# A macaron block on one core: the order of work in an attention step, one small copy moved to another engine, fewer products of constants

## The chip, the cores and the metric

The kernel runs on one core of a Trainium2 chip. The metric is the device time of one execution in microseconds, as the median of several runs. The engines named below are TensorE (PE, with its weight loads PEld), VectorE (DVE), ScalarE (ACT), GpSimd (POOL) and SyncE (SP), which here only issues DMAs.

## What is computed

The input `x` has 4 sequences of 2048 tokens with 256 features, so 8192 tokens, all float32. The block is a macaron: half a mixture-of-experts layer, attention, and half a mixture-of-experts layer again, with the same weights in both halves.

```python
x = x + 0.5 * ffn(layernorm(x))
x = x + attention(layernorm(x))
x = x + 0.5 * ffn(layernorm(x))

def attention(x):                      # H = 16 heads of 16 features
    s = (16 ** 0.5) ** -0.25
    q = split_heads(x @ Wq + bq)
    v = split_heads(x @ Wv + bv)
    q = softmax(q, axis=-1) * s        # over the 16 features of a head
    k = softmax(q, axis=-2) * s        # over the 2048 tokens, from q
    ctx = einsum('bhnd,bhne->bhde', k, v)
    return merge(einsum('bhnd,bhde->bhne', q, ctx)) @ Wo + bo
```

`ffn` routes each token to 2 of 8 experts by a softmax over `x @ router_w.T`. An expert takes at most 1280 tokens, those with the largest weights first. It computes `(silu(x @ wg) * (x @ wu)) @ wd` with 1024 hidden features, and the weighted results are added to the token's row.

## The kernel before

**Stages.** In the profiled execution the first router and the routing take the first 103 us. The first experts' products run from about 107 to 922 us, attention from 922 to 1160 us, the second routing to about 1223 us, and the second experts to the end. The experts gather the rows of their tokens with indirect DMAs on GpSimd's queue (`gather`), transpose them on TensorE, multiply, and scatter the results with indirect DMAs.

**Products of constants.** `stay_busy(out, n, cols)` issues n matrix products of constants that nothing reads. There are seven of them ahead of attention. In each of the two experts' stages there are four of 512 columns behind the first two gathers, and one of 384 columns behind each of the first two transposes of gathered rows.

**Attention in tiles and pairs.** The 8192 tokens are 64 tiles of 128 tokens; a tile is one slice `xw[:, t, :]` in SBUF. Two tiles make a pair, so there are 32 pairs (`NP`), and 8 pairs make a sequence (`PB`). The tiles are loaded from DRAM four at a time (`JL`), by 16 DMAs of 512 KB on SP's queue, in order. Besides the 256 features a tile of `xw` has 8 more columns: `wqx` is `Wq` with the router's weights beside it, so that the projection of the unnormalized tile also gives its part of the next router's logits (`W1` is 264 columns).

**The loop.** `attention` runs a loop of 44 steps. It stands in a manual schedule, so every engine executes its instructions in the order in which they are written, and no planner moves them. Step `i` works on several pairs at once, each at its own stage:

- `stats(2i+2)`: mean and variance of the next pair on VectorE; GpSimd makes the reciprocal deviation `rstd`.
- `turn_x(i)`: four transposes of the pair (`trx`) on TensorE, and a ScalarE copy out of PSUM to `xT`.
- `project(i-1)`: eight products into `qp` (PSUM, one buffer).
- `logits_in(i-1)`: a ScalarE copy of 128x16 logits from `qp` into `xw`.
- `largest(i-1)`: VectorE scales `qp` into `q` (two instructions) and takes the largest value of each head (`m`); GpSimd subtracts it from `q` in place.
- `exp(i-2)`: the exponential of `q` on ScalarE, in place. `share(i-2)`: VectorE sums each head (`z`) and takes the reciprocal (`rz`); GpSimd multiplies `q` by it in place. Here `q` holds the softmax.
- `keys(i-3)`: ScalarE takes a second exponential, `ek`, and scales the two tiles of the pair by `rstd` into a ring of four buffers (`xs`).
- `turn_q(i-3)`: four transposes of `q` (`trq`) and a ScalarE copy to `qT`.
- `sums(i-3)`: eight products of `ek` and `xs`, added up in `pc` over the 8 pairs of a sequence.
- `add_y(i-12)`: eight products of `qT` and the sequence's context `mo` into `py` (PSUM, one buffer until the last pairs). `take_y`: VectorE adds `py` to `xw`, takes the new statistics, and every second time the normalization constants (`norm_of`).
- `choose_on`: VectorE's part of the routing of finished tiles (`choose`), in small portions, from step 20 on.

When the 8 pairs of a sequence are summed, four parts make its context. `context_1` (steps 11, 19, 27, 35) takes the reciprocal `rc` on VectorE and scales `pc` into `g`, half on ScalarE and half on VectorE. `context_2` transposes `g` (`trg`) and copies it to `gT` on ScalarE. `context_3` multiplies it by the weights of `v` (`ctx`) and scales it on VectorE. `context_4`, in the next step, multiplies by `Wo` and makes `mo`.

**Buffers.** `trx`, `trq`, `trg` and `ctx` share the tag `tr`, which has two PSUM buffers. They are handed out in the order in which the code asks for them, and each comes free when the copy of its contents has been made. The tag `q` has five buffers in SBUF, `m` and `z` three.

**Order within a step.** The body of the loop sets it. Before the change it is: `context_1`, `context_4`, `exp`, `turn_x`, `share`, `stats`, `project`, `logits_in`, `keys`, `context_2`, `largest`, `turn_q`, `add_y`, `context_3`, `sums`, `choose_on`, `take_y`. In the sequence with the last context (step 35) portions of `choose_on` stand between them.

Of the kernel before, what the change touches and what calls it, by code (L numbers as in the profile page):

```python
# [26 lines left out]
def macaron_kernel(  # L27
# [22 lines left out]
    nc = tc.nc  # L50
# [3 lines left out]
    T = B * NJ  # L54
# [96 lines left out]
    def stay_busy(ps, n, cols=BANK):  # L151

        for _ in range(n):
            nc.tensor.matmul(ps[:, :cols], ident, row_of_ones[:, :cols], start=True, stop=True)

    def spread(ap, shape):
        return ap.to_broadcast(shape)
# [280 lines left out]
    def experts(name, src, dst, wait_for, weights, wpool, pool, ppool):  # L438
# [33 lines left out]
        def turn(k, q):  # L472

            if k >= len(chunks):
                return
            if q == 0:
                turned[k] = xTs[k] = pool.tile([P, DC, CH * P], F32, tag="xsT", name="xsT", bufs=2)
            c, i0, i1 = q // 2, (0, TURN)[q % 2], (TURN, CH)[q % 2]
            ps = ppool.tile([P, BANK], F32, tag="tr", name="tr", bufs=1)
            for i in range(i0, i1):  # L480
                nc.tensor.transpose(  # L481
                    ps[:, (i - i0) * P : (i - i0 + 1) * P], got[k][i][:, c * P : (c + 1) * P], ident
                )
                if k == 0 and c == 0 and i + 1 < TURN:
                    stay_busy(banks()[:, 0, :], 1, BANK * 3 // 4)
            nc.scalar.copy(turned[k][:, c, i0 * P : i1 * P], ps[:, : (i1 - i0) * P])

        def tt(o, a, b, op):
# [26 lines left out]
        def banks():  # L515

            return ppool.tile([P, 2, BANK], F32, tag="mm", name="mm", bufs=3)
# [138 lines left out]
        with tc.manual_schedule(engines=ENGINES - {mybir.EngineType.Pool}):  # L656
            first.high()
            first.begin()
            for g in range(NL):
                first.low(g)  # L660
                first.products(g)
            first.sum()
            lists[0] = first.end()
            gather(0)
            gather(1)
            stay_busy(banks()[:, 0, :], 4)
            for m in range(2):
                sums_of_w(0, m)
            blank(0, *range(TURN))
            for q in (0, 2):  # L670
                turn(0, q)
            for k, (e, i0) in enumerate(chunks):
                for p, hs in enumerate(steps_of(k)):
                    beside(k, p)

                order = [(i, p, j) for i in range(CH) for p in range(NF) for j in range(2)]
                order = sorted(order[: 4 * NF], key=lambda o: (o[1] == NF - 1, o[0])) + order[4 * NF :]
                po = {}
                for i, p, j in order:
                    if i not in po:  # L680

                        po[i] = banks()[:, 0, :D]
                    nc.tensor.matmul(  # L683
                        po[i], hs[p][:, j, i * P : (i + 1) * P], weights[e][2][:, j * NF + p, :],
                        start=(p == 0 and j == 0), stop=(p == NF - 1 and j == 1),
                    )
                    if i == CH - 1 and (p, j) == (NF // 2, 0):
                        behind(k, i - 0.5)
                    if p < NF - 1 or j == 0:
                        continue  # L690
                    eo = pool.tile([P, D], F32, tag="eo", name="eo", bufs=6)
                    nc.scalar.mul(eo, po[i], got[k][i][:, D + e : D + e + 1])  # L692
                    ins = nc.gpsimd.indirect_dma_start(  # L693
                        out=dst[:, :],
                        out_offset=bass.IndirectOffsetOnAxis(ap=lists[e][:, i0 + i : i0 + i + 1], axis=0),
                        in_=eo, in_offset=None, compute_op=ALU.add,
                    )
                    tc.declare_no_dep(ins.ins, group=f"{name}{e}", reason="an expert's rows are distinct")
                    tc.add_to_no_dep_group(f"{name}{e}", ins.ins)
                    after(ins, sent[e - 1], "the rows' earlier sums")  # L700
                    sent.setdefault(e, []).append(ins)
                    behind(k, i)
                del got[k]
                if i0 + CH == ST:
                    load_expert(e + 2, wpool, weights)
# [68 lines left out]
    def attention(xw, w, to, weights, pool, ppool):  # L774
# [34 lines left out]
                    )  # L809
            del xT[i]  # L810

        def logits_in(i):
            nc.scalar.copy(xw[:, 2 * i : 2 * i + 2, D:W1], qp[i][:, :, D:W1])

        def largest(i):
            q = pool.tile([P, 2, D], F32, tag="q", name="q", bufs=5)
            for k in range(2):
                nc.vector.scalar_tensor_tensor(  # L818
                    q[:, k, :], qp[i][:, k, 0:D], rstd[:, 2 * i + k : 2 * i + k + 1], bqs, ALU.mult, ALU.add
                )  # L820
            qs[i] = q.rearrange("p k (h d) -> p (k h) d", d=H)
            m = pool.tile([P, 2 * H], F32, tag="m", name="m", bufs=3)
            nc.vector.tensor_reduce(m, qs[i], AX.X, ALU.max)  # L823
            nc.gpsimd.tensor_tensor(qs[i], qs[i], spread(m.unsqueeze(2), [P, 2 * H, H]), ALU.subtract)  # L824

        def exp(i):
# [9 lines left out]
        def keys(i):  # L836


            eks[i] = pool.tile([P, 2, D], F32, tag="ek", name="ek", bufs=3)
            nc.scalar.activation(  # L840
                eks[i].rearrange("p k (h d) -> p (k h) d", d=H), qs[i], AF.Exp, scale=QSCALE
            )
            for k in range(2):
                t = 2 * i + k
                nc.scalar.mul(ring[i % 4][:, k, 0:D], xw[:, t, 0:D], rstd[:, t : t + 1])

        def turn_q(i):
            ps = ppool.tile([P, DC, 2, P], F32, tag="tr", name="trq", bufs=2)
# [119 lines left out]
        def has(i, n=NP):  # L968
            return 0 <= i < n

        LAST = NP + PB + 4
        with tc.manual_schedule(engines=ENGINES):
            stay_busy(ppool.tile([P, 2, 2 * D], F32, tag="py", name="py", bufs=1)[:, 0, :], 7)
            stats(0, 2)
            for i in range(LAST):
                y = i - PB - 4

                b3 = (i - 3) // PB - 1 if (i - 3) % PB == 0 else -1
                b4 = (i - 4) // PB - 1 if (i - 4) % PB == 0 else -1
                if has(b3, B):  # L980
                    context_1(b3)
                if b3 == B - 1:
                    choose_on(1, 0)
                if has(b4, B - 1):
                    context_4(b4)
                if has(i - 2):
                    exp(i - 2)
                if has(i):
                    turn_x(i)
                if has(i - 2):  # L990
                    share(i - 2)
                if has(i + 1):
                    stats(2 * i + 2, 2)
                if has(i - 1):
                    project(i - 1)
                    logits_in(i - 1)
                if has(i - 3):
                    keys(i - 3)
                if has(b3, B):
                    context_2(b3)  # L1000
                if b3 == B - 1:
                    choose_on(1, 0)
                if has(i - 1):
                    largest(i - 1)
                if has(i - 3):
                    turn_q(i - 3)
                ps = add_y(y) if has(y) else None
                if b3 == B - 1:
                    choose_on(3, 0)
                if has(b3, B):  # L1010
                    context_3(b3)
                if b3 == B - 1:
                    choose_on(2, 0)
                    context_4(b3)
                if has(i - 3):
                    sums(i - 3)
                if i < LAST - PB - 2:
                    choose_on(2, 2)
                if has(y):
                    take_y(y, ps)  # L1020
                if i >= LAST - PB:

                    choose_on({LAST - 3: 0, LAST - 2: 5, LAST - 1: 3}.get(i, 4), 0)
            while choosing:
                for k in reversed(range(len(choosing))):
                    choose_on(1, 0, k)
            for ts, _, tiles in chosen:
                for t in tiles:
                    norm_row(xw, t)
                write_rows(xw, to, ts)  # L1030
# [98 lines left out]
    xw = kept.tile([P, T, W], F32, name="xw")  # L1129
    w = kept.tile([P, E, T], F32, name="w")  # L1130
    with tc.tile_pool(name="at", bufs=1) as pool, tc.tile_pool(name="atp", bufs=1, space=PSUM) as ppool:
        for t in range(0, T, JL):
            nc.sync.dma_start(out=xw[:, t : t + JL, 0:D], in_=acc_tiles[:, t : t + JL, :])
        attention(xw, w, rows[1], att_weights, pool, ppool)


# [41 lines left out]
```

## Time and profile before

| what | value |
|---|---|
| time, median of 3 runs | 2049.84 us (2045.59 to 2050.16) |
| profiled execution: its own time | 2049.3 us |
| profiled execution: span of the trace | 2047.4 us |
| granted TensorE clock, mean | 0.959 of full speed |
| PE busy | 1891.1 us (92% of the span) |
| PEld busy | 1443.5 us (71%) |
| DVE busy | 1413.7 us (69%) |
| POOL busy | 883.5 us (43%) |
| ACT busy | 656.7 us (32%) |

The span is the time from the first to the last recorded instruction of the execution; 1.9 us of the execution's own time lie around it. Busy shares are averages over all stages, and the stages have different limits. In the experts' stages PE's slices of the span are at 90% or more, while in the attention stage (slices 19 to 23 of 40) they are lower at the beginning and in the routing behind it. So the change has to be read from the trace of the attention stage, step by step, and not from these totals. In a row of the trace a line such as L827 is the line of the program that issued the instruction, and `out<-in` gives the names of its tiles.

### The profile page before, as it was taken

Reading aid. Unit: us, or ns where it says so; the run is one execution under the profiler, and the core shown is the slowest. Engines: PE = TensorE matmul, PEld = TensorE weight load, DVE = VectorE, ACT = ScalarE, POOL = GpSimd, SP = SyncE. Lnnn points to the kernel's source line nnn. Section 1 sums busy time; section 2 is a strip of 40 time slices with the busy share of each in tenths; the row PEclk is TensorE's granted clock in tenths of the full one; section 3 lists DMA queues with packets and bytes.
Section 4 is the critical chain, followed back from the end, with each engine's and each line's share of the span. In section 5 each row is a group of like instructions: output and inputs, shape, how many; then the busy total and the mean of one; then the engine's idle time right before and its main releaser. Section 6 shows DMA issues by size and latency. Waiting matters only on the chain.

```text
span 2047.4 us, 24768 instructions
## 1 busy us (share of the span) xinstructions
PE 1891.1 (92%) x9200; PEld 1443.5 (71%) x9200; DVE 1413.7 (69%) x2499; ACT 656.7 (32%) x1357; POOL 883.5 (43%) x737
## 2 busy tenths in 40 slices
PE   6289999999999999997999628999999999999998
PEld 4257777777777777775888415777777777777776
DVE  7867676767676767545789886767676766767654
ACT  5322323222223222224566503222322222223221
POOL 5335353535353535334556303535353535353533
PEclk8579999999999999999999858999999999999999
DMA  9912222222231322115012531223132323131211
GB/s 350 298 28 38 78 38 78 40 77 64 52 79 37 79 40 39 18 16 169 21 42 86 181 136 28 71 45 79 37 79 40 81 37 83 35 84 35 42 15 13
DMA packets 99911, 147.63 MB, mean 72 GB/s; under 512 B 7496, under 2 KB 86352, under 8 KB 99664
## 3 DMA queue, kind: packets, MB, share of 16 engines
q1 hardware_dynamic: 69056, 102.77, 14.9%
q0 software_dynamic: 30720, 43.27, 13.0%
q8 instruction: 73, 1.20, 0.3%
q14 instruction: 46, 0.38, 0.1%
q10 hardware_dynamic: 16, 0.01, 0.0%
HBM read 98.84 MB, written 55.57 MB: 75 GB/s over the span
## 4 chain that ended last, share of the span: by engine, by line
PE 82%; DVE 7%; POOL 2%; issue 1%; ACT 1%; DMA 1%; POOLq 0%; SPq 0%; DVEq 0%; ACTq 0%
PE mm L536 41%; PE mm L683 27%; PE one L536 7%; PE tr L481 2%; PE ix L404 1%; PE py L922 1%; DVE above L303 1%; PE pc L864 1%; PE qp L807 1%; DVE q L818 1%; POOL q L824 1%; DVE m L823 1%; DVE z L831 1%; DVE st L934 0%; DVE st L791 0%
## 5 line engine op out<-in xcount | busy, mean ns | idle before, releaser
L683 PE MATMUL mm<-wdt,h 128*128 128x256 f32 x2560 | 579.0, 381 | 0.0
L683 PEld LDWEIGHTS mm<-wdt,h 128*128 128x128 f32 x2560 | 475.9, 190 | 63.9
L568 POOL TENSOR_TENSOR h<-ct 128x1280 f32<-128x1280 f32 x96 | 279.2, 2908 | 423.6 <-ACT ct L565 420.4
L536 PE MATMUL mm<-xs,ws 128*128 128x320 f32 x1536 | 459.5, 435 | 2.0 <-DVE xs L489 2.0
L489 DVE TENSOR_TENSOR ct<-ct,mm 128x640 f32<-128x640 f32 x384 | 313.1, 818 | 104.3 <-PE mm L536 96.2
L536 PEld LDWEIGHTS mm<-xs,ws 128*128 128x128 f32 x1536 | 292.4, 191 | 127.4 <-issue 6.6
L565 ACT ACTIVATE ct<-ct 128x320 f32<-128x320 f32 (+1 forms) x224 | 181.8, 812 | 283.7 <-DVE ct L489 283.7
L489 DVE TENSOR_TENSOR ct<-p,mm 128x640 f32<-128x640 f32 x128 | 105.1, 821 | 238.5 <-ACT p L553 200.5
L489 DVE TENSOR_TENSOR ct<-u,mm 128x640 f32<-128x640 f32 x256 | 210.3, 821 | 58.3 <-PE mm L536 55.3
L553 ACT COPY p<-one 128x320 f32<-128x320 f32 x256 | 108.8, 425 | 406.2 <-PE one L536 404.0
L693 POOL DMA_INDIRECT out_dram<-eo,ixs x80 | 133.1, 1664 | 220.7 <-ACT eo L692 213.7
L693 POOL DMA_INDIRECT acc<-eo,ixs x80 | 132.8, 1660 | 221.1 <-ACT eo L692 214.1
L456 POOL DMA_INDIRECT r<-rows,ixs x160 | 159.1, 994 | 145.4 <-DVE ws L489 97.3
L692 ACT ACTIVATE eo<-mm,r 128x256 f32<-128x256 f32 x160 | 75.9, 474 | 396.3 <-PE mm L683 396.3
L536 PE MATMUL mm<-xsT,ws 128*128 128x320 f32 x512 | 158.7, 432 | 0.0
L395 DVE TENSOR_TENSOR lo<-count,slot_lo 128x1024 f16<-128x1024 int16 x112 | 128.3, 1218 | 0.0
L536 PEld LDWEIGHTS mm<-xsT,ws 128*128 128x128 f32 x512 | 97.3, 190 | 40.5
L489 DVE TENSOR_TENSOR u<-p,mm 128x640 f32<-128x640 f32 x128 | 104.9, 820 | 16.4 <-PE mm L536 13.3
L536 PE MATMUL mm<-xsT,wgt 128*128 128x320 f32 x256 | 91.0, 437 | 0.0
L536 PE MATMUL one<-xsT,wgt 128*128 128x320 f32 x256 | 91.0, 437 | 0.0
L536 PE MATMUL mm<-xsT,wut 128*128 128x320 f32 x256 | 90.9, 437 | 0.0
L536 PE MATMUL one<-xsT,wut 128*128 128x320 f32 x256 | 90.1, 434 | 0.0
(211 smaller groups left out, 2333.6 us busy)
## 6 DMA issues: line engine op xcount, KB each, us to landing
wgt<-in_L_ffn_wg_dram SPq DMA_DIRECT2D x16, 1024.0 KB, 5.0
wut<-in_L_ffn_wu_dram SPq DMA_DIRECT2D x16, 1024.0 KB, 7.0
wdt<-in_L_ffn_wd_dram SPq DMA_DIRECT2D x16, 1024.0 KB, 5.6
rows<-xw SPq DMA_DIRECT2D x7, 2176.0 KB, 11.1
xw<-in_L_attn_x_dram SPq DMA_DIRECT2D x16, 512.0 KB, 8.9
xw<-acc SPq DMA_DIRECT2D x16, 512.0 KB, 8.8
out_dram<-xw SPq DMA_DIRECT2D x16, 512.0 KB, 2.9
r<-rows,ixs POOLq DMA_INDIRECT x160
```

Source lines behind the costliest of these rows:

```text
L303: nc.vector.tensor_scalar(above, wt, cand_f, 0.0, ALU.is_ge, ALU.add, accum_out=part)
L395: nc.vector.tensor_tensor(lo, spread(count.unsqueeze(1), shape), spread(at.unsqueeze(2), shape), ALU.is_equal)
L456: nc.gpsimd.indirect_dma_start(out=r, out_offset=None, in_=src[:, :], in_offset=bass.IndirectOffsetOnAxis(ap=lists[e][:, i : i + 1], axis=0),)
L481: nc.tensor.transpose(ps[:, (i - i0) * P : (i - i0 + 1) * P], got[k][i][:, c * P : (c + 1) * P], ident)
L489: nc.vector.tensor_tensor(o, a, b, op)
L536: nc.tensor.matmul(ps, a, b, start=True, stop=True)
L553: nc.scalar.copy(p1[p][:, m, :], one[:, :BH])
L565: nc.scalar.activation(ct[:, qs, 0, :], ct[:, qs, 0, :], AF.Silu)
L568: engine.tensor_tensor(hq[:, qs, :], ct[:, qs, 0, :], ct[:, qs, 1, :], ALU.mult)
L683: nc.tensor.matmul(po[i], hs[p][:, j, i * P : (i + 1) * P], weights[e][2][:, j * NF + p, :], start=(p == 0 and j == 0), stop=(p == NF - 1 ...
L692: nc.scalar.mul(eo, po[i], got[k][i][:, D + e : D + e + 1])
L693: ins = nc.gpsimd.indirect_dma_start(out=dst[:, :], out_offset=bass.IndirectOffsetOnAxis(ap=lists[e][:, i0 + i : i0 + i + 1], axis=0), in_ ...
```

## The change

In the loop the order becomes: `context_1`, `context_4`, `project`, `largest`, `keys`, `exp`, `share`, `stats`, `turn_q`, `turn_x`, `context_2`, `add_y`, `context_3`, `sums`, `choose_on`, `take_y`. So the projection and the largest of pair i-1 stand first, the exponential and the sum of pair i-2 behind them, and the transposes of `q` and of the next pair behind the projection.

The logits are copied by VectorE, behind the reduction `m` and ahead of GpSimd's subtraction, where before ScalarE copied them (`logits_in`). In `keys` the two scalings stand ahead of the exponential.

The first load of the attention stage is split into two of two tiles each, so there are 17 loads.

The products of constants in the two experts' stages are gone; the seven ahead of attention stay.

```diff
@@ in the experts: turning the gathered rows, and their start @@
-                if k == 0 and c == 0 and i + 1 < TURN:
-                    stay_busy(banks()[:, 0, :], 1, BANK * 3 // 4)
...
             gather(0)
             gather(1)
-            stay_busy(banks()[:, 0, :], 4)
@@ in attention @@
-        def logits_in(i):
-            nc.scalar.copy(xw[:, 2 * i : 2 * i + 2, D:W1], qp[i][:, :, D:W1])
-
         def largest(i):
...
             nc.vector.tensor_reduce(m, qs[i], AX.X, ALU.max)
+            nc.vector.tensor_copy(xw[:, 2 * i : 2 * i + 2, D:W1], qp[i][:, :, D:W1])
             nc.gpsimd.tensor_tensor(qs[i], qs[i], spread(m.unsqueeze(2), [P, 2 * H, H]), ALU.subtract)
@@ keys @@
+            for k in range(2):
+                t = 2 * i + k
+                nc.scalar.mul(ring[i % 4][:, k, 0:D], xw[:, t, 0:D], rstd[:, t : t + 1])
             eks[i] = pool.tile([P, 2, D], F32, tag="ek", name="ek", bufs=3)
             nc.scalar.activation(
                 eks[i].rearrange("p k (h d) -> p (k h) d", d=H), qs[i], AF.Exp, scale=QSCALE
             )
-            for k in range(2):
-                t = 2 * i + k
-                nc.scalar.mul(ring[i % 4][:, k, 0:D], xw[:, t, 0:D], rstd[:, t : t + 1])
@@ the loop @@
+                if has(i - 1):
+                    project(i - 1)
+                    largest(i - 1)
+                if has(i - 3):
+                    keys(i - 3)
                 if has(i - 2):
+
                     exp(i - 2)
-                if has(i):
-                    turn_x(i)
-                if has(i - 2):
                     share(i - 2)
                 if has(i + 1):
                     stats(2 * i + 2, 2)
-                if has(i - 1):
-                    project(i - 1)
-                    logits_in(i - 1)
                 if has(i - 3):
-                    keys(i - 3)
+                    turn_q(i - 3)
+                if has(i):
+                    turn_x(i)
                 if has(b3, B):
                     context_2(b3)
                 if b3 == B - 1:
                     choose_on(1, 0)
-                if has(i - 1):
-                    largest(i - 1)
-                if has(i - 3):
-                    turn_q(i - 3)
                 ps = add_y(y) if has(y) else None
@@ the loads of attention @@
-        for t in range(0, T, JL):
-            nc.sync.dma_start(out=xw[:, t : t + JL, 0:D], in_=acc_tiles[:, t : t + JL, :])
+        for t, n in [(0, 2), (2, 2)] + [(t, JL) for t in range(JL, T, JL)]:
+            nc.sync.dma_start(out=xw[:, t : t + n, 0:D], in_=acc_tiles[:, t : t + n, :])
```

## The prediction

> **What bounds the kernel now.** I read three views of the trace: time by stretch, the chain of waits through the attention stage, and the timelines of single steps. Page and chain put two thirds of the run on the experts' products (L536, L683), which the change leaves alone but for a few products at each start; attention runs from 922 to 1160 us. The chain of waits there (start, length, what ran) shows two regimes. In an early step:
>
> ```profile
> 969.84 0.64 ACT q L827
> ...
> 970.50 0.70 DVE z L831
> ...
> 971.22 0.35 DVE rz L833
> ...
> 972.52 0.87 DVE q L818 x2
> ...
> 973.41 0.70 DVE m L823
> ...
> 974.25 1.07 POOL q L824
> ...
> 975.34 0.64 ACT q L827
> ```
>
> This is a ring over three engines: VectorE issues `m`, idles while POOL subtracts and ScalarE exponentiates, and only then sums (`z`). It costs 975.34 - 969.84 = 5.50 us a step, with TensorE partly idle. From step 12 on, when `py` joins, the chain is TensorE alone:
>
> ```profile
> 999.75 1.78 PE qp L807 x8
> 1001.53 0.44 PE trq L852 x4
> 1001.97 1.78 PE py L922 x8
> 1003.75 1.74 PE pc L864 x8
> 1005.49 0.44 PE trx L799 x4
> 1005.92 1.78 PE qp L807 x8
> ```
>
> That is 6.17 us a step without a gap, and it lasts almost to the end of the projections: qp starts at 993.41 in step 12, 1045.02 in step 20, 1098.04 in step 28. From step 20 `choose` fills VectorE as well. A table by stretch (length; busy time with instruction count of PE, PEld, DVE, ACT, POOL; clock; DMA) shows how full:
>
> ```profile
> 1054.33:1061.28 6.95, 6.95 (x37) 6.02 (x36) 6.64 (x21) 4.89 (x12) 3.74 (x8) 1.00 0.24 79
> ```
>
> VectorE trails TensorE there: in step 26 its `q` starts at 1087.14, 3.1 us after qp ended. In step 27 TensorE first stops for it:
>
> ```profile
> 1090.75 0.33 PE L886 MATMUL trg<-ident,g 128*128 128x128 f32 x1 [0.56 <-ACT g L877]
> ```
>
> **What the Trainium skill says.** "SBUF — State Buffer", Who interferes with whom: a VectorE instruction with two SBUF inputs and a GpSimd one that reads SBUF exclude each other. The timeline agrees: the same small operation takes 0.16 us alone and 0.81 us during POOL's 1.07 us subtraction (the third line):
>
> ```profile
> 1148.22 0.16 DVE L223 SCALAR_TENSOR_TENSOR sm<-rs,b 128x12 f32<-128x12 f32 x1
> ...
> 1069.42 0.81 DVE L223 SCALAR_TENSOR_TENSOR sm<-rs,b 128x16 f32<-128x16 f32 x1
> ...
> 1069.13 1.07 POOL L824 TENSOR_TENSOR q<-q,m 128x512 f32<-128x512 f32 x1 [0.41 <-DVE m L823]
> ```
>
> "TensorE: Matmul & The Clock Gate", Architectural detail: ScalarE, VectorE and GpSimd run strictly in order, so whatever stands behind a waiting instruction waits too. The ring above is an instance. Same page, Part 1: the clock follows windows of some 3.4 us of activity. The stretches agree (1.00 at 117, 0.50 from 121 to 125, 1.00 at 127, 0.50 at 131 us).
>
> **Early steps (1 to 11): gain.** `largest` now stands before `share` of the pair before it, whose subtraction has run during the previous step. The ring is open; what is left is TensorE's 0.44 + 1.78 + 0.44 + 1.74 = 4.40 us. I lay one step out from qp's start at 0, with start-to-start distances from the timelines. `q` starts at 1.98, `m` 2.87, the logits copy 3.48, `z` 3.60, `rz` 4.32, statistics to 5.62. POOL's subtraction runs 3.65 to 4.72, its multiplication 4.75 to 5.82, and `trq` of the next step needs that at 4.40 + 1.78 = 6.18: it fits by 0.36 us. The copy on VectorE has a near row, a 128x16 copy out of PSUM (L1103), 0.174 us; I take 0.12 start to start, with 0.05 to 0.3 as ends. qp has one buffer, so its next use waits for this copy, 3.70 us after qp's start: covered. ScalarE loses a 0.17 us copy and does xs, ek, exp, qT, xT in 3.0 us: covered. Keys' scalings ahead of its exponential cost nothing, since the exponential would wait for POOL's multiplication meanwhile.
>
> The first load is halved, one issue more on SP (1.19 us apart). At the 351 GB/s of 930 to 940 us half of 512 KB is 0.75 us earlier, so qp(0) starts near 930.75 instead of 931.64. The later loads land one place later, long before their steps. qp(1) and qp(2) follow at 3.70 us (934.45, 938.15), qp(3) at 942.95 after waiting for POOL's first multiplication; then seven steps of 4.39 us give qp(10) at 973.7. Step 11 has the context: `rc` waits on VectorE until 1.25, ScalarE's `g` 1.45, xs 1.93, ek 2.73, exp 3.26, qT 3.80 to 4.37, and `trg` only behind it (below); with gT, ctx, pc and mops qp(11) comes 9.2 us later, at 982.9. Before: 993.41. **Gain 10.5 us**, ends 8.5 and 11.5.
>
> **Middle (12 to 18): nothing.** TensorE sets 6.17 in both. VectorE needs 5.15 us a step and 5.62 with norm_of, POOL about 4.
>
> **The context steps: loss.** The transposes share two PSUM buffers. Before, the order trx, qp, trg, trq gave `trg` a long free one. Now trq, trx, trg follow each other, and `trg` takes the buffer that ScalarE's qT copy has to empty. That copy stands behind `g`, both xs, ek and exp, and `g` behind VectorE's `rc`. Step 19: VectorE ends step 18 at 0.96, `rc` 1.0, `g` 1.2, xs 1.68, ek 2.48, exp 3.01, qT 3.55 to 4.12, `trg` at 4.17 instead of 2.66: **1.5 us lost**. py, ctx, pc and the next qp queue behind it.
>
> **Late (20 to 34): loss.** VectorE's step is 5.15 + choose (0.6 to 1.6) + 0.47 every second time, above 6.17 on average. Before, `z`, `rz` and the statistics (2.0 us) could run before qp was ready, so VectorE could trail by 3 us without harm. Now all stands behind `q`: the add of `y` that frees py's only buffer ends at 1.98 + 4.34 + choose, and the next py wants it at 6.17 + 2.66, so a lag over some 1.2 us stops TensorE. `choose` also moves from behind `m` to behind the statistics, into POOL's multiplication instead of its subtraction: blocked likewise. Carrying the lag from step to step (`q` late by 0, 0, 1.2, 1.6, 2.0, 2.3, 2.5 us in steps 20 to 26) gives 0.85 us of stops, and step 27 reaches `rc` 2.6 us after qp's start; the ScalarE queue of step 19 then ends 3.05 us after `trg` could start, where 0.75 was lost before. From qp(19) to qp(27): 55.5 against 53.0, **2.5 lost**. Steps 28 to 34 likewise: pc of step 34 ends at 41.6 against 38.8 after qp(27), **2.8 lost**. Ends for the context and late steps together: 2 and 13. From step 35 the work is the same.
>
> **Products of constants.** Two stages lose 4 of 3.60 to 3.73 us in all and 2 of 0.81 and 1.49. They run while TensorE waits for gathered rows: the third transpose starts at 121.50 behind the last of them, when its row was ready at 121.43. Under 0.1 us. The clock was at 0.50 in spite of them when the first expert products ran (123.23), so no warmth is lost; but the later stage's place in the clock's windows shifts, worth up to 2 us either way.
>
> **Sum.** -10.5 + 1.5 + 2.5 + 2.8 = -3.7 us on the profiled execution (2049.3; 2047.4 span and 1.9 around it), which is 0.5 below the median shown: 2045.6.
>
> **Rivals.** *The gain stays*: VectorE's lag stays under the allowance and the context steps cost 3 us in all: -10.5 + 3 = -7.5, 2041.8. For it: components of VectorE's step overlap. Against: before, in steps 20 to 25, its steps average 6.6 us. *The copy blocks* (slower): the logits copy stands exactly where POOL starts subtracting; if it were held for that 1.07 us, VectorE's step is 6.1 in the middle and 7.1 or more late: 13 late steps lose 13 us more, the early ones 0.3 each (3), the middle 2: 2045.6 + 18 = 2064. It decides from a copy of about 0.75 us. Against: it has one input, in PSUM, and `m` and `z` pass POOL's work unchanged at 0.69. *The ring is not opened*: POOL's multiplication misses the 0.36 us and `trq` waits: steps of about 5, gain 5 instead of 10.5, 2051.
>
> **Numbers.** A measurement of this kernel can tell about 0.3% from no change, 6.1 us. Main line 0.55, gain stays 0.27, ring not opened 0.09, copy blocks 0.09. Some of the main line lies past the edge: faster 0.32, same 0.59, slower 0.09. Range: best -11.5 + 2 = -9.5, worst -8.5 + 13 = +4.5 before the rare rivals, and the runs shown lie 4.6 us apart, up to 4.3 below their median: 2038 to 2053.
>
> **What would show it.** Right: early steps of 4.4 us with `z` no longer waiting for ScalarE, TensorE near full; qp(11) some 10 us earlier; `trg` waiting for a ScalarE copy in steps 19 and 27; py waiting for VectorE's add from step 22. Wrong: early steps still above 5, py and trg without stops, or a copy above 0.5 us.

## The result and the profile after

The changed kernel runs in 2040.71 us (median, 2038.74 to 2043.93), beside 2047.33 us for the kernel before on the same chip. The ratio is 0.997, with a 95% interval of 0.9959 to 0.9981. On another chip it was 0.9978 (0.9969 to 0.9986), so by the two ratios the change is worth 4.5 to 6 us. (A ratio is taken over all runs and need not be the quotient of the two medians.) 2045.6 against 2049.3, a ratio of 0.998, was predicted.

The two profiled executions lie 10.5 us apart (spans 2047.4 and 2036.9), more than the medians. Cut at the same instructions, the difference lies here:

| stretch of the profiled execution | before | after | difference |
|---|---|---|---|
| start to the first index product (`ix`) | 107.34 | 105.96 | -1.4 |
| to the 33rd product of `xs` and `ws`, first experts | 43.70 | 41.20 | -2.5 |
| to their last product of `wdt` and `h` | 770.17 | 769.35 | -0.8 |
| to the first `qp` | 10.43 | 9.40 | -1.0 |
| to the last `pc` | 204.97 | 199.78 | -5.2 |
| to the first transposed row of the second experts | 98.28 | 99.28 | +1.0 |
| to the end | 812.48 | 811.88 | -0.6 |

So attention with its load and the routing behind it (-1.0, -5.2 and +1.0) gives -5.2 us, in line with the ratios. The start of the run has no edit in it. The start of the first experts moves by 2 to 3 us from one profile to the next of any kernel here; the experiments show why.

The chain of waits in an early step of the kernel after (start, length, what ran) is TensorE alone:

```profile
947.55 1.78 PE qp L804 x8
949.34 0.44 PE trq L847 x4
949.77 0.44 PE trx L796 x4
950.21 1.74 PE pc L859 x8
951.95 1.78 PE qp L804 x8
```

One qp starts 4.40 us after the other, where a step of 5.50 stood before. VectorE's timeline shows the order and the price of the moved copy:

```profile
958.23 0.88 DVE L812 SCALAR_TENSOR_TENSOR q<-qp,rstd,bqs 128x256 f32<-128x256 f32 x2 [0.35 <-PE qp L804]
959.13 0.69 DVE L817 TENSOR_REDUCE m<-q 128x32 f32<-128x512 f32 x1
959.74 0.17 DVE L818 COPY xw<-qp 128x16 f32<-128x16 f32 x1
959.82 0.68 DVE L826 TENSOR_REDUCE z<-q 128x32 f32<-128x512 f32 x1
```

Now `q` waits for TensorE, and `z` follows `m` without a wait for ScalarE. The copy takes 0.17 us and delays `z` by 0.08. TensorE's timeline of step 27 shows the loss on the other side; in brackets, the idle time and what ended it:

```profile
1076.63 0.60 PE L847 MATMUL trq<-ident,q 128*128 128x128 f32 x4
1077.07 0.60 PE L796 MATMUL trx<-ident,xw 128*128 128x128 f32 x4
1079.83 0.66 PE L881 MATMUL trg<-ident,g 128*128 128x128 f32 x4 [2.16 <-ACT qT L849]
1080.32 1.95 PE L917 MATMUL py<-mo,qT 128*128 128x264 f32 x8
```

The distances between the starts of qp, before and after: step 11 8.15 and 9.23 us, step 19 8.39 and 9.68, step 27 9.80 and 10.77. Between them every step is 6.17 in both kernels. The gain of 10.0 us from qp(0) to qp(10) is the largest it gets, and 3.3 of it go back in the three context steps.

### The profile page after: what moved, and what is told of

It is laid out like the page before. It is cut to its first block, busy times and chain, and to the rows that moved or that the text cites. A ratio compares the mean times of both kernels' runs of the same rounds, so it can differ in the third digit from the quotient of the medians.

```text
span 2036.9 us, 24719 instructions
## 1 busy us (share of the span) xinstructions
PE 1875.8 (92%) x9176; PEld 1440.3 (71%) x9176; DVE 1417.6 (70%) x2531; ACT 657.1 (32%) x1325; POOL 883.1 (43%) x737
## 4 chain that ended last, share of the span: by engine, by line
PE 83%; DVE 5%; issue 4%; ACT 1%; POOL 1%; DMA 1%; POOLq 0%; DVEq 0%; ACTq 0%; SPq 0%
PE mm L534 41%; PE mm L680 27%; PE one L534 7%; PE tr L481 2%; PE qp L804 1%; PE pc L859 1%; PE ix L404 1%; PE py L917 1%; DVE st L929 1%; DVE xw L927 1%; DVE q L812 1%; DVE m L817 0%; DVE z L826 0%; DVE st L788 0%; PE trq L847 0%
```

## Experiments

Three questions were put: which edit carries the early gain, where the profile's other differences come from, and what the context steps lose.

### The parts one by one

`attn_only` is the changed kernel with the constants and the whole first load put back:

```diff
...
+            stay_busy(banks()[:, 0, :], 4)
...
-        for t, n in [(0, 2), (2, 2)] + [(t, JL) for t in range(JL, T, JL)]:
+        for t in range(0, T, JL):
```

> The changed kernel with the products of constants put back in both experts' stages and the first load whole again, so only the order of the loop, the logits copy and the order in keys differ from before. Theory A (the attention stage carries the change): steps 4 to 10 take 4.39 us, trg waits for qT in steps 19 and 27, and from the first qp to the second routing's products the time is 4.2 us less than before (5.2 in the pair of profiles, less 1.0 for the load); in the runs -4.2 us, ratio 0.998. Theory B (the experts' stages carry most of it, by the place of the clock's windows): the runs show under 2 us less than before, ratio 0.999 or more. Rival to both: the whole load at the start makes the early steps wait again, and the first steps lose more than 1 us.

Measured: 2044.79 us, ratio 0.9993 (0.9984 to 1.0002). The early steps are at 4.39 as expected, and steps 19 and 27 at 9.67 and 10.77. But step 11 took 10.88 us where the changed kernel took 9.23. The table by stretch (length; busy time of PE, PEld, DVE, ACT, POOL; granted clock; DMA) shows why:

```profile
974.20:977.60 3.40, 1.27 (x10) 0.80 (x9) 3.30 (x10) 3.14 (x7) 1.89 (x3) 1.00 0.00 0
977.60:981.00 3.40, 3.40 (x13) 3.03 (x14) 0.86 (x4) 1.64 (x4) 1.33 (x3) 0.50 0.00 0
```

TensorE's timeline has two stops in the first row:

```profile
976.12 0.66 PE L884 MATMUL trg<-ident,g 128*128 128x128 f32 x4 [1.45 <-ACT qT L852]
977.46 1.96 PE L896 MATMUL ctx<-gT,wvx 128*128 128x128 f32 x8 [0.68 <-ACT gT L886]
```

So it is busy for 1.27 of the 3.40 us there, and the next 3.4 us run at half clock: `pc` takes 2.81 us instead of 1.90. The step is 1.65 us longer than in the changed kernel with the same stops. The granted clock changes by windows of 3.4 us; one at half clock is called slow here. In the profile of the changed kernel the two stops fell across the edge of two windows:

```profile
970.40:973.80 3.40, 1.96 (x13) 1.51 (x12) 2.78 (x9) 2.82 (x7) 1.72 (x4) 1.00 0.02 5
973.80:977.20 3.40, 2.70 (x17) 2.36 (x18) 2.28 (x8) 2.90 (x6) 2.82 (x4) 1.00 0.00 0
```

Neither is under half busy, and the clock stays at 1.00. Over the fourteen profiles, from 115 to 2030 us, all 42 windows at full clock in which TensorE was busy for under 0.4 were followed by one at half clock, and 26 of the 37 between 0.4 and 0.5, 2 of 33 between 0.5 and 0.6, and none of the 7372 above. The Trainium skill ("TensorE: Matmul & The Clock Gate", Part 1) says that the window is 3413 ns and free-running, and that its place varies from run to run. The records here agree: the lengths are 3.413 us and multiples, and they lie differently in each profile.

The number of the runs alone is on the side of theory B: the interval holds 1, and in the profile the time from the first qp to the second routing's products is 2.4 us less than before, where 4.2 was expected. The early steps are the gain of theory A; the profile shows 1.65 us of it lost by the slow window in step 11. How often such a window falls there in other executions is not on record.

`const_only` is the kernel before with the two edits to `stay_busy` alone:

```diff
-                if k == 0 and c == 0 and i + 1 < TURN:
-                    stay_busy(banks()[:, 0, :], 1, BANK * 3 // 4)
...
-            stay_busy(banks()[:, 0, :], 4)
```

> The kernel before without the products of constants in the two experts' stages, nothing else changed. Theory A: the 2.3 us that the first experts' start was shorter in the pair of profiles is the chance place of the clock's windows (3.41 us each); the runs show 0 to -1 us, ratio 0.9995 to 1.0, and the profile may show the slow windows in the first products in either number (none to two). Theory B: the constants themselves wake the clock too early and cost a later slow window; the runs show -2 to -4 us (two stages), ratio 0.998 to 0.999, and the start of both stages (first ix product to the 33rd product of xs and ws) is 2 us shorter than before. Rival: without the constants the first products run at half clock for longer, and the runs show +1 us or more.

Measured: 2047.54 us, ratio 1.0002 (0.9994 to 1.001). From the first index product to the 33rd product of `xs` and `ws` it took 43.00 us. Over all profiles this stretch is 41.6 to 43.7 us with the constants and 41.2 to 44.5 without. In the nine without it goes with the windows at half clock some 22 us behind the first index product: 41.2 to 41.3 us with none there, 43.0 to 43.3 with one, 44.5 with two. The kernel before has one there, the changed kernel none. So most of the 2.5 us in the pair of profiles is the place of the windows; some tenths may be the constants.

`load_only` is the kernel before with the split load alone:

```diff
-        for t in range(0, T, JL):
+        for t, n in [(0, 2), (2, 2)] + [(t, JL) for t in range(JL, T, JL)]:
```

> The kernel before with the first load of attention in two halves, nothing else changed. From the last product of the first experts to the first qp 9.4 us instead of 10.43, if the 1.0 us of the pair of profiles is the load's; 10.4 if it came from the order (project ahead of the other work). The rest of attention as before.

Measured: 9.23 us, and 9.24 to 9.40 in every other kernel with the split load, against 10.41 to 10.58 in every one without. The load is worth 1.2 us in the mean of these. In the old order most of it is lost at once: the step to qp(1) is 0.9 us longer than before (4.30 against 3.38), since `q` there stands behind statistics that wait for the second load. In the changed kernel nothing is lost: with the whole load (`attn_only`) and the split one that step is 3.98. Another 0.9 us of `load_only`'s attention, in step 3, goes with a slow window at 936 us; its single time, 2046.1 us, tells nothing more.

`with_const` is the changed kernel with the constants put back as in `attn_only`, its load still split.

> The changed kernel with the products of constants put back in both experts' stages: the new order with the split load. The order alone gave 2044.8, the changed kernel 2040.7, and taking the constants alone out of the kernel before gave nothing. If the split load is worth its 1.0 us and the constants nothing, this runs at -2 to -4 against before, ratio 0.998 to 0.999, and the rest of the 6 us is the spread of runs with the place of the clock's windows. If the constants are worth 2 us or more in the new kernel, it is at 0.999 or above, 2 us or more over the changed kernel; if the load is worth much more than 1 us, it is at 0.997.

Measured: 2045.29 us, ratio 0.9986 (0.9978 to 0.9995), and its profile has slow windows in steps 11 and 27 (10.90 and 12.45 us). `after_again` is the changed kernel beside later ones.

> The changed kernel itself, on the same chip as the others of this call. With the constants kept it ran at 0.9986, with constants and the whole load at 0.9993. If removing the constants is worth nothing here either, the earlier 0.997 was on the lucky side and this shows 0.998 to 0.9985; if they are worth 2 us or more in the new kernel, 0.9965 to 0.9975.

Measured: 2044.79 us, ratio 0.9978 (0.9969 to 0.9986), between the two expectations; in its profile every step has the length of the first within 0.03 us. The intervals with and without constants overlap; the ratios themselves lie 1.6 to 3.3 us apart. So removing the constants may be worth some 3 us in the new kernel or nothing; this is not settled, and with it how the 4.5 to 6 us divide between the order, the load and the constants.

### What carries the early gain

`sum_first` puts `exp` and `share` back ahead of `project` and `largest`:

```diff
+                if has(i - 2):
+                    exp(i - 2)
+                    share(i - 2)
                 if has(i - 1):
                     project(i - 1)
                     largest(i - 1)
                 if has(i - 3):
                     keys(i - 3)
-                if has(i - 2):
-                    exp(i - 2)
-                    share(i - 2)
```

> The changed kernel with the exponential and the sum of pair i-2 put back ahead of the projection and largest of pair i-1, nothing else. If the early gain is the opened ring (m, subtraction, exponential, z, q, m), steps 4 to 10 are back at 5.2 to 5.5 us instead of 4.39, z waits for ScalarE again, and the late steps keep 6.17. If the early gain came from somewhere else (the transposes behind the projection, the copy on VectorE), they stay below 4.8.

Measured: 4.39 us in steps 4 to 10, so the expectation fell: once the statistics stand behind `m`, as here, the order of `largest` and `share` is not needed for the gain. The ring is there again, as the chain of waits shows:

```profile
958.78 0.64 ACT q L822
...
959.44 0.70 DVE z L826
...
960.43 0.80 DVE q L812 x2
...
961.25 0.69 DVE m L817
...
962.09 1.07 POOL q L819
...
963.18 0.64 ACT q L822
```

But the statistics now stand behind `m` and no longer between `rz` and `q`. Without them the ring takes 963.18 - 958.78 = 4.40 us, no more than TensorE's own products, so nothing is lost. The old place of `exp` and `share` even helps elsewhere: the context steps are 8.29, 9.03 and 9.38 us against 9.23, 9.68 and 10.77, and from the first qp to the last pc the profile is 3.8 us shorter than the changed kernel's. This is one execution (2040.88 us), so what it is worth in time is open.

`stats_behind` makes that single edit, the place of the statistics, in the kernel before:

```diff
-                if has(i + 1):
-                    stats(2 * i + 2, 2)
                 if has(i - 1):
                     project(i - 1)
...
                 if has(i - 1):
                     largest(i - 1)
+                if has(i + 1):
+                    stats(2 * i + 2, 2)
```

> The kernel before with one edit: the statistics of pair i+1 (about 1.2 us on VectorE) moved from behind the sum z to behind largest; the order of everything else, the copy on ScalarE, the constants and the load as before. Theory C (the ring of m, subtraction, exponential, z, rz, statistics, q, m was long because the statistics stood in it): early steps fall from 5.43 to 5.50 us to 4.4 to 4.6, the ring now 4.3; the context steps keep the order trx, qp, trg and stay at 8.1, 8.4 and 9.8, so all of the 10 us is kept and the kernel runs 8 to 10 us below before, ratio 0.9955. Theory D (it takes the projection ahead of the exponential, or largest ahead of share): early steps stay above 5.2, ratio 0.999 to 1.0. Between them: pc waits for the scalings xs behind ek as it did before (1.4 us a step), early steps near 5.

Measured: 2046.13 us, ratio 0.9989 (0.9981 to 0.9998), and early steps of 5.41 us, hardly shorter than the 5.43 to 5.50 before. (Step 27 is 8.72 for 9.80.) That is the number of theory D, but the chain of waits names another bound than its reason:

```profile
966.57 1.80 PE qp L807 x8
968.36 0.02 issue
968.38 0.17 ACT xw L813
968.56 0.53 ACT ek L840
969.09 0.41 ACT xs L845
969.49 0.04 issue
969.54 2.00 PE pc L864 x8
971.54 0.44 PE trx L799 x4
971.97 0.23 PE qp L807
```

This is a second ring, through ScalarE's queue: the logits copy can't run before qp has ended; `ek` and the first `xs` stand behind it; `pc` needs them; and `trx` and the next qp stand behind `pc`. It takes 5.41 us, nearly as much as the first. In the profile of the kernel before, the waits from 941 to 985 us (engine, what for, total, times, longest) had shown both:

```profile
DVE z L831 <- ACT q L827: 14.9, 8, 1.9
...
PE pc L864 <- ACT xs L845: 7.5, 8, 1.4
```

`copy_on_act` is the changed kernel with the logits copy back on ScalarE, behind the projection:

```diff
             del xT[i]
+            nc.scalar.copy(xw[:, 2 * i : 2 * i + 2, D:W1], qp[i][:, :, D:W1])
...
-            nc.vector.tensor_copy(xw[:, 2 * i : 2 * i + 2, D:W1], qp[i][:, :, D:W1])
```

> The changed kernel with the logits copy back on ScalarE, behind the projection and so ahead of keys, nothing else. With the statistics out of the first ring the kernel before still had early steps of 5.41 us, in a second ring: qp, the copy on ScalarE, ek, xs, pc, trx, qp. If that copy holds ScalarE's queue until qp has ended, then here the scalings and ek end 1.8 + 0.17 + 0.8 + 0.53 = 3.3 us after qp's start, pc starts there instead of at 2.66, and steps 4 to 10 take 5.0 to 5.1 us instead of 4.39; middle and late steps keep 6.17 (py stands ahead of pc); the kernel runs 5 to 7 us above the changed one, ratio to before 1.0 to 1.001. If the copy costs its 0.17 us on ScalarE and no more, as the prediction had it, the steps stay at 4.4 to 4.5 and the ratio at 0.9975 to 0.998.

Measured: 2055.88 us, ratio 1.0039 (1.002 to 1.0059), slower than the kernel before, with early steps of 5.37 us (5.0 to 5.1 expected) and this chain:

```profile
964.05 1.79 PE qp L804 x8
965.84 0.02 issue
965.86 0.17 ACT xw L808
966.03 0.72 ACT xs L836 x2
966.75 0.61 ACT ek L838
967.37 0.04 issue
967.41 2.00 PE pc L859 x8
969.41 0.67 PE qp L804 x3
```

One copy of 0.17 us on the wrong engine costs 1.0 us in each early step, because of what it waits for and what stands behind it. Step 19 grows too (10.31 us), since `trg` waits for the end of the same queue, and step 11 (11.14), where a window at half clock follows the stops as in `attn_only`. By the ratios the kernel is some 12 to 14 us above the changed one, where 5 to 7 were expected; its profile is 12.5 us longer from the first qp to the last pc, 7.5 of it in the steps up to 10.

So the early gain needs both rings out of the way. The copy on VectorE opens the second, which this single edit shows. The first is open in the changed kernel by the order, as predicted; in `sum_first` it is closed, but short enough by the place of the statistics. The kernel before with the copy alone on VectorE was not run; that it would stay at about 5.5 us is argued from the first ring's chain.

### What the context steps lose

`trg_first` puts `context_2` directly behind `largest`:

```diff
                     largest(i - 1)
+                if has(b3, B):
+                    context_2(b3)
                 if has(i - 3):
                     keys(i - 3)
```

> The changed kernel with context_2 (the transposes trg and the copy gT) directly behind largest, ahead of keys, so that trg takes the buffer that the trq of the step before used, and no longer the one that this step's qT copy has to empty. If trg's wait for the qT copy is what the context steps lose, steps 19 and 27 (8.4 us of products each) fall from 9.68 and 10.77 us to about 8.6 and 9.5 (what is left is g, late behind rc on VectorE), step 11 from 9.23 to about 8, and the whole by 3 us against the changed kernel, -9 against before, ratio 0.9955. If the loss is g's own lateness behind VectorE, step 27 stays above 10 us and the whole within 1 us of the changed kernel.

Measured: 2041.4 us, ratio 0.9974 (0.9964 to 0.9983), no better than the changed kernel; steps 19 and 27 took 9.46 and 10.56, not the 8.6 and 9.5 expected, and step 11 took 11.30 with a slow window in it. In step 11, on TensorE:

```profile
976.70 0.66 PE L796 MATMUL trx<-ident,xw 128*128 128x128 f32 x4 [0.24 <-ACT gT L883]
979.01 1.78 PE L893 MATMUL ctx<-gT,wvx 128*128 128x128 f32 x8 [1.66 <-ACT qT L849]
```

The stop has moved from `trg` to `ctx`: with two buffers, the second request behind `trq` gets the one that the qT copy has to empty, whoever it is. `late_trx` therefore leaves one request less there:

```diff
-                if has(i):
+                if has(i) and not has(b3, B):
                     turn_x(i)
                 if has(b3, B):
                     context_2(b3)
...
                 ps = add_y(y) if has(y) else None
...
+                if has(i) and b3 in (1, 2):
+                    turn_x(i)
+                if b3 == 0:
+                    sums(i - 3)
                 if has(b3, B):
                     context_3(b3)
+                if b3 == 0:
+                    turn_x(i)
...
-                if has(i - 3):
+                if has(i - 3) and b3 != 0:
                     sums(i - 3)
```

> The changed kernel, in the three context steps with pairs to come alone (11, 19, 27): turn_x behind add_y (in step 11 behind context_3, with sums ahead of context_3), so that trg takes the buffer of the trx before, free for a whole step, and the copies qT and gT are made while py runs. If the loss in the context steps is the order of the tr buffers against ScalarE's queue, trg starts behind trq without a stop in step 19 and waits only for g in step 27: steps of 7.0, 8.5 and 9.1 us instead of 9.23, 9.68 and 10.77, and 5 us less than the changed kernel, ratio to before 0.9945. If only the place of a stop moves, as with trg ahead of keys (9.46 and 10.56), the steps stay above 9.4 and 10.5 and the whole at the changed kernel's 0.997.

Measured: 2037.54 us, ratio 0.9948 (0.9935 to 0.9961); steps of 7.61, 8.39 and 9.33, together 4.35 us less than in the changed kernel. In step 27 `trg` waits for `g` alone:

```profile
1075.26 0.33 PE L881 MATMUL trg<-ident,g 128*128 128x128 f32 x1 [0.30 <-ACT g L872]
1075.78 0.55 PE L881 MATMUL trg<-ident,g 128*128 128x128 f32 x3 [0.19 <-DVE g L873]
```

`late_trx_rc` adds `context_1` at the end of the step before:

```diff
-                if has(b3, B):
-                    context_1(b3)
...
+                if (i - 2) % PB == 0 and has((i - 2) // PB - 1, B):
+                    context_1((i - 2) // PB - 1)
                 if has(y):
                     take_y(y, ps)
```

> As the one with trx late, and context_1 (rc and g) moved from the start of the context step to the end of the step before, ahead of take_y, so that rc no longer stands behind VectorE's add of y and two statistics. If VectorE's lag is what is left in step 27, that step falls from about 9.1 to 8.5 us as step 19, and the whole is 0.5 us below the other; if the lag is not at work there, the two are alike. On the other side, the add of y comes 0.6 us later in steps 10, 18 and 26; if py stops for it, step 27 or 28 is longer.

Measured: 2039.21 us, ratio 0.9954 (0.9941 to 0.9967), not told apart from the one without it. Step 27 is 8.93 and step 19 8.60: 0.4 us won and 0.2 lost. In step 27 `mops` now waits 0.30 us for the later add of `y`; what step 19 loses to is not named in its trace.

`sum_first_late` joins the orders of `sum_first` and `late_trx`.

> The changed kernel with exponential and sum of pair i-2 ahead of projection and largest, and with trx late in the context steps. The first alone had early steps of 4.39 us and context steps of 8.29, 9.03 and 9.38; trx late alone 7.61, 8.39 and 9.33. If the two work on different waits, step 27 falls to about 8.5 (trg waits for neither qT nor VectorE's lag) and the kernel is 0.5 to 1 us below trx late, ratio to before 0.994. If the exponential ahead of g and xs puts gT and ek later, steps 11 and 27 grow by up to 0.5 us and it is the same as trx late or 1 us slower.

Measured: 2034.81 us, ratio 0.9929 (0.9915 to 0.9942), the lowest of all; it is clear of the changed kernel, and its interval overlaps that of `late_trx`. Early steps are at 4.39, the context steps at 7.19, 8.39 and 8.39 us, and TensorE has no stop in step 27:

```profile
1077.77 0.60 PE L847 MATMUL trq<-ident,q 128*128 128x128 f32 x4
1078.21 0.60 PE L881 MATMUL trg<-ident,g 128*128 128x128 f32 x4
1078.64 1.95 PE L917 MATMUL py<-mo,qT 128*128 128x264 f32 x8
```

## Why the prediction was right, and where it was not

The time lay in the stated range and the direction was right. The early gain and the context steps came out nearly as laid down. The size of the late loss, and the reason of the early gain, did not. The stated time stood on 2049.3 us for the kernel before, 2.0 above its median beside the change, so the differences are what to compare: -3.7 stated, -4.5 to -6 measured.

**Early steps: right in size, half right in reason.** qp(1) and qp(2) came after 3.98 and 3.95 us (3.70 stated), step 3 took 4.76, the others 4.39 but one, and step 11 9.23 (9.2 stated). With the load, qp(11) gained 9.95 us against 10.5. But the step "the ring is open; what is left is TensorE's" 4.40 us failed as an account. There were two rings, of 5.50 and 5.41 us, and opening the first alone (`stats_behind`) gave 1.9 us up to qp(10), 1.1 of it in step 2. What the prediction costed at nothing, ScalarE "loses a 0.17 us copy", is the edit that opens the second, and without it (`copy_on_act`) the kernel is slower than before. The sum held all the same, by luck and not by its reasoning, because the laid-out step had the copy in its new place. Whether the scalings `xs` ahead of `ek` matter was not tried alone.

**The load.** 0.9 us stated, 1.2 measured.

**The context steps.** `trg` waits for the qT copy in steps 19 and 27, as stated. Step 19 lost 1.3 us (1.5 stated). The stop in step 27 is 2.16 us (3.05 stated).

**The late steps: the term that was mis-sized.** From qp(19) to qp(27) 1.0 us were lost (2.5 stated), and from qp(27) to the last pc 1.5 (2.8 stated). The failed step is VectorE's length: the working let `q` fall behind by up to 2.5 us in steps 20 to 26, with 0.85 us of stops of `py` besides, some 0.56 us a step above 6.17 (an estimate from these two terms). The distance from qp's start to `q` grew from 1.98 us in step 21 to 3.14 at most, so the lag stayed at 1.2 or less, and no `py` stopped. The six steps from 21 to 26 by stretch, first before and then after:

```profile
1051.20:1088.24 37.04, 37.04 (x194) 32.01 (x193) 34.46 (x101) 25.35 (x57) 22.67 (x38) 1.00 0.18 61
```

```profile
1037.83:1074.85 37.02, 37.02 (x193) 32.31 (x192) 35.52 (x108) 25.99 (x53) 23.18 (x40) 1.00 0.15 50
```

VectorE is busy for 35.52 of 37.02 us (third of the five busy times). From one `q` to the next its steps are 6.35 us on average: above 6.17, as stated, but by 0.18. `choose` takes 0.64 to 1.35 us of such a step in steps 20 to 25, 0.86 on average (1.03 before), and nothing in step 26. The stated lag asks for some 1.3 a step (an estimate: 6.17 and 0.56, less the stated 5.15 and half of 0.47), so the price of `choose` had been put too high. The add of `y` ended at most 8.53 us after qp's start, and the next py wants it at 6.17 + 2.66 = 8.83, so only 0.3 us were left.

Of the 1.5 us behind qp(27), 0.4 stand in step 31, because one `trx` more falls behind qp(27) in the new order, and 1.1 in step 33. There no projection is left to stand ahead of `trq`, and it waits for POOL's multiplication:

```profile
1117.49 0.66 PE L847 MATMUL trq<-ident,q 128*128 128x128 f32 x4 [1.29 <-POOL q L829]
```

All this is near the mechanism of the rival "the gain stays": its -7.5 stands beside the -6.2 us from the last product of the first experts to the last pc.

**What took 1 us back.** Behind the last pc the kernel after was 1.0 us longer, which no step had. The work there is the same, and so is its longest stop (`py` waits 1.50 us for VectorE in both). But a window at half clock, from 1134.2 to 1137.6 us, fell on the products. Over the fourteen profiles the stretch from the last pc to the first transposed row is 99.3 to 99.7 us in the five with such a window ahead of the routing's long stretch at half clock, and 97.9 to 98.3 in the other nine. So the 1.0 us is the place of a window and not the edit.

**Constants.** "Under 0.1 us" is not contradicted in the kernel before (1.0002, 0.9994 to 1.001) and is open in the new one. The windows did shift the start of the stages, as chance from run to run.

**The other rivals.** The copy did not block: 0.17 us beside POOL's subtraction. The ring did open, and `trq` did not wait in the steps of 4.39; it waited for POOL only in step 33.

## What to carry to other kernels

Before pricing an edit at nothing because it removes a short instruction, ask what that instruction waits for and what stands behind it in its queue; a step can be held by two rings of nearly equal length, and then opening one alone is worth little (1.9 us here) and both together all of it (10.0). The view of waits shows the second ring before the first is opened: every line of it that recurs once a step is a candidate. Where buffers go round, the order of requests decides which copy the next one waits for, and asking later for the buffer that is not urgent (`late_trx`) can beat asking earlier for the urgent one (`trg_first`).

## What the runs showed of the hardware beyond what was expected

A window of 3.4 us at full clock is followed by one at half clock if TensorE was busy for under 0.4 of it, in most cases up to 0.5, and hardly above. Two stops of 1.45 and 0.68 us within one window were enough, and cost 1.65 us more. By the place of the windows, which differs from run to run, stretches with the same instructions differ: step 11 by 1.7 us, the start of the first experts without constants by up to 3.3, the stretch behind attention by up to 1.8. So a pair of single profiles can differ by more than the edits in them (10.5 us here, against 4.5 to 6).
